# Column-tiled pairs of attention heads in layer 1, row ends shared between VectorE and GpSimd, and node sums laid into the last rows

## Chip, cores and metric

The kernel runs on one core of a Trainium2 chip. The metric is the device time of one execution in microseconds (us). Engines are called PE (matmul), PEld (weight load), DVE (VectorE), ACT (ScalarE), POOL (GpSimd) and SP (SyncE, here only a DMA queue).

## The reference, cut to what matters

Four layers on a graph of 2708 nodes with 256 features, each with a residual and a layer norm. The change is in layer 1, and in the passage from it to layer 2.

```python
# layer 1: masked attention, 4 heads of 64
h = (x @ W).reshape(n, heads, head_dim)
src = einsum('nhd,d->nh', h, a[:head_dim, 0]);  dst = einsum('nhd,d->nh', h, a[head_dim:, 0])
e = leaky_relu(src[:, :, None] + dst.T[None])          # slope 0.2
attn = softmax(where(adj > 0, e, -9e15), axis=-1)
out = einsum('nhm,mhd->nhd', attn, h).reshape(n, 256)
out = (out - mean) / sqrt(var + 1e-5) * gamma + beta
x = layernorm(x + out)
# layer 2 starts with: row statistics of the edge attention (min, then sum of exp, 3 heads),
#   node_support = (adj without diagonal) @ x, and a GRU cell on it
```

Nodes are cut into 22 row blocks of 128 (the last has 20 rows) and into six column groups (four of 512, one of 384, one of 276). "Row ends" are what is left of layer 1 for a row block when its sums are there: division by the softmax total, two normalisations, the residual. "Logits" are the small products of the finished rows that layer 2 needs. "Node sums" are the support matmuls of layer 2.

## The kernel before

For each column group and each head, DVE makes the unnormalised attention tile p (128 x 512), and PE multiplies it by the head's 64 features plus a 65th column of ones, which gives the softmax total. A scheduler fixes the order of every engine's instructions when the kernel is compiled; the engines then run their lists in order.

```python
for lo, hi in spans:                       # six column groups
    for h in range(H):
        acc = ps_acc.tile([P, 512], F32, tag="acc", name="acc")
        for c in range(NT):                # 22 chunks
            p = l1.tile([P, W], F32, tag="p", name="p", bufs=6)
            nc.vector.scalar_tensor_tensor(p[:, :w], fall_b[:, h, at : at + w], rise[:, c, h : h + 1],
                                           mask[:, c, at : at + w], ALU.max, ALU.mult)
            nc.tensor.matmul(acc[: HD + 1, :w], hs[c][:, h, :], p[:, :w], start=(c == 0), stop=(c == NT - 1))
            # ... every fifth chunk: one row block's logits
        # ... copy of the sums; after head 0: layer1_end of the group before, its elementwise work all on DVE,
        #     but for the power step of the norm, which is on GpSimd
```

The softmax here doesn't subtract the row's maximum and nothing guards it: scores larger than these inputs give would overflow.

## Time and profile before

2139.2 us is the median of three runs. The costliest groups that the change touches, from the page (name of the group, then busy us, mean ns of one, and idle time before it with what ended it):

```profile
L504 PE MATMUL acc<-p,h 128*65 128x512 f32 (+2 forms) x1056 | 417.8, 548 | 13.9 <-DVE p L500 12.8
L500 DVE SCALAR_TENSOR_TENSOR p<-fall_b,rise,mask 128x512 f32<-128x512 f32 (+2 forms) x528 | 354.4, 684 | 25.6 <-PE acc L504 2.1
```

Layer 1's matmuls take 418 us of PE, and DVE's p takes 354 us beside them. PE uses 65 of the 128 columns of its array. The prediction below shows the stages:

| stage of before | us | ends at |
|---|---|---|
| layer 1 proper | 466 | 728.5 |
| last rows, to the logits in DRAM | 26 | 755 |
| wait, then first pass of the row statistics | 34 | 789.3 |
| row statistics (66 passes on DVE) | 270 | 1059.5 |
| the rest | 1084 | 2144 |

### The profile page before, as it was taken

The page shows a single profiled execution, that of the slowest core. Times are in us where ns is not written, and L with a number is a line of the kernel's source. Part 1 is how long each engine was busy: PE and PEld are TensorE (multiplying, and loading weights), DVE is VectorE, ACT ScalarE, POOL GpSimd, SP SyncE. Part 2 cuts the span into 40 slices and gives each one's busy share as a digit, 9 for nine tenths or more (in the row PEclk, how much of TensorE's full clock was granted, in tenths as well). Part 3 has the DMA queues.
Part 4 walks back from the last instruction along what each step waited for, and adds up shares of the span by engine and source line. Part 5 has one row for each costly group of instructions (what it writes and reads, how often), then busy time and mean ns, then how long its engine had stood idle before and what let it go on. Part 6 is the DMA issues. An engine that isn't in the chain of part 4 may idle for free.

```text
span 2144.2 us, 18986 instructions
## 1 busy us (share of the span) xinstructions
PE 2058.3 (96%) x6618; PEld 1122.7 (52%) x6618; DVE 1342.5 (63%) x2721; ACT 694.3 (32%) x951; POOL 175.2 (8%) x286
## 2 busy tenths in 40 slices
PE   8999999999999889999889999999999999999997
PEld 7888633333234334445544444444444546678885
DVE  4333398989999739999856646646646557542111
ACT  0100145654111317767733333323323334320000
POOL 0111110120110110000000000000000000001111
PEclk9999999999999889999999999999999999999999
DMA  7344333331000297766380401301201101015452
GB/s 264 127 144 163 124 135 111 132 111 59 10 8 3 81 319 225 231 223 193 92 250 0 138 7 44 117 20 49 81 22 53 45 22 40 18 62 180 175 189 100
DMA packets 172564, 234.20 MB, mean 109 GB/s; under 512 B 18109, under 2 KB 149339, under 8 KB 161795
## 3 DMA queue, kind: packets, MB, share of 16 engines
q1 hardware_dynamic: 159738, 180.98, 26.5%
q0 software_dynamic: 9792, 47.51, 6.3%
q10 hardware_dynamic: 2928, 4.41, 0.6%
q8 instruction: 54, 0.88, 0.2%
q14 instruction: 52, 0.42, 0.1%
HBM read 221.63 MB, written 11.23 MB: 109 GB/s over the span
## 4 chain that ended last, share of the span: by engine, by line
PE 51%; DVE 5%; ACT 3%; issue 2%; SPq 2%; DMA 2%; POOL 0%; POOLq 0%; DVEq 0%; ACTq 0%
PE acc L801 20%; PE acc L178 9%; PE gate L584 8%; PE s L643 7%; PE gate L745 3%; PE pz L191 2%; ACT p L798 2%; SPq L170 2%; DVE p L795 2%; DMA blk<-in_adj_t_dram 1%; DVE z L682 1%; DVE p L799 1%; ACT z L687 1%; PE tr L141 0%; DMA strip<-in_adj_t_dram 0%
## 5 line engine op out<-in xcount | busy, mean ns | idle before, releaser
L801 PE MATMUL acc<-p,x 128*128 128x512 f32 (+2 forms) x1584 | 614.0, 544 | 6.2 <-DVE p L799 6.2
L801 PEld LDWEIGHTS acc<-p,x 128*128 128x128 f32 x1584 | 296.2, 190 | 298.7 <-issue 212.7
L504 PE MATMUL acc<-p,h 128*65 128x512 f32 (+2 forms) x1056 | 417.8, 548 | 13.9 <-DVE p L500 12.8
L178 PE MATMUL acc<-turn,strip 128*128 128x256 f32 (+1 forms) x1804 | 397.9, 379 | 1.4 <-DMA strip<-in_adj_t_dram 1.4
L500 DVE SCALAR_TENSOR_TENSOR p<-fall_b,rise,mask 128x512 f32<-128x512 f32 (+2 forms) x528 | 354.4, 684 | 25.6 <-PE acc L504 2.1
L178 PEld LDWEIGHTS acc<-turn,strip 128*128 128x128 f32 (+1 forms) x1804 | 331.2, 186 | 54.8 <-DMA strip<-in_adj_t_dram 1.8
L798 ACT ACTIVATE p<-p 128x512 f32<-128x512 f32 (+2 forms) x396 | 226.9, 578 | 401.5 <-DVE p L795 387.6
L799 DVE TENSOR_TENSOR p<-p,blk 128x512 f32<-128x512 f32 (+2 forms) x396 | 246.4, 626 | 169.8 <-ACT p L798 165.7
L504 PEld LDWEIGHTS acc<-p,h 128*65 128x65 f32 x1056 | 140.4, 139 | 256.7 <-issue 120.7
L687 ACT ACTIVATE z<-z,st 128x2708 f32<-128x2708 f32 (+1 forms) x66 | 168.4, 2552 | 102.7 <-DVE st L682 100.6
L682 DVE CUSTOM_DVE_ANT_0 z<-e_b,none 128x2708 f32<-128x2708 f32 (+1 forms) x66 | 195.4, 2967 | 0.3
L795 DVE TENSOR_SCALAR p<-st_b,e_col 128x512 f32<-128x512 f32 (+2 forms) x396 | 175.7, 448 | 15.8 <-PE acc L801 14.9
L134 POOL TENSOR_TENSOR bn_rs<-bn_ve,neg_half 128x1 f32<-128x1 f32 (+1 forms) x110 | 73.9, 674 | 1264.5 <-DVE bn_ve L132 1227.6
L643 PE MATMUL s<-blk,x 128*128 128x512 f32 (+2 forms) x416 | 165.5, 558 | 8.2 <-ACT supt L649 8.2
L584 PE MATMUL gate<-xt,whh 128*128 128x512 f32 (+2 forms) x288 | 123.5, 552 | 9.1 <-DMA xt<-xt 8.1
L643 PEld LDWEIGHTS s<-blk,x 128*128 128x128 f32 x416 | 80.9, 195 | 91.0 <-issue 69.3
L143 ACT COPY xt<-tr 128x256 f32<-128x256 f32 x66 | 23.8, 361 | 273.7 <-PE tr L141 266.7
L830 DVE SCALAR_TENSOR_TENSOR o<-acc,rdeg,o 128x256 f32<-128x256 f32 (+1 forms) x22 | 10.6, 483 | 144.3 <-PE acc L178 144.3
L584 PEld LDWEIGHTS gate<-xt,whh 128*128 128x128 f32 x288 | 55.8, 195 | 64.6 <-issue 45.0
L481 ACT ACTIVATE turn<-turn 128x2708 f32<-128x2708 f32 (+1 forms) x22 | 54.1, 2461 | 93.9 <-DMA turn<-in_adj_dram 93.9
L278 DVE TENSOR_SCALAR mask<-strip 128x2816 fp8e4<-128x2816 f32 (+3 forms) x37 | 36.7, 998 | 61.1 <-DMA strip<-in_adj_t_dram 60.9
L596 DVE SCALAR_TENSOR_TENSOR g_r<-g_r,g_h 128x512 f32<-128x512 f32 (+2 forms) x24 | 15.0, 626 | 92.2 <-ACT g_h L589 92.2
(147 smaller groups left out, 1400.6 us busy)
## 6 DMA issues: line engine op xcount, KB each, us to landing
strip<-in_adj_t_dram SPq DMA_DIRECT2D x41, 1408.0 KB, 6.1
blk<-in_adj_t_dram SPq DMA_DIRECT2D x189, 256.0 KB, 4.8
turn<-in_adj_dram SPq DMA_DIRECT2D x21, 1354.0 KB, 5.8
arow<-in_adj_dram POOLq DMA_DIRECT2D x21, 1354.0 KB, 7.0
st_b<-st_d SPq DMA_DIRECT2D x4, 1536.0 KB, 7.3
turn<-in_adj_t_dram SPq DMA_DIRECT2D x21, 256.0 KB, 7.0
blk<-in_adj_t_dram SPq DMA_DIRECT2D x36, 128.0 KB, 2.6
fall_b<-fall_d POOLq DMA_DIRECT2D x4, 1024.0 KB, 6.1
```

The lines of the kernel that those rows point to most:

```text
L134: nc.gpsimd.tensor_tensor(rstd[:n], ve[:n], neg_half[:n], ALU.pow)
L178: nc.tensor.matmul(acc, s[:, c, :n], rhs(c), start=(c == 0), stop=(c == NT - 1))
L500: nc.vector.scalar_tensor_tensor(p[:, :w], fall_b[:, h, at : at + w], rise[:, c, h : h + 1], mask[:, c, at : at + w], ALU.max, ALU.mult,)
L504: nc.tensor.matmul(acc[: HD + 1, :w], hs[c][:, h, :], p[:, :w], start=(c == 0), stop=(c == NT - 1))
L584: nc.tensor.matmul(g[:, :w], lt, rt, start=(q == 0), stop=(q == len(terms) - 1))
L643: nc.tensor.matmul(acc[f][:, :w], xs[c][:, f * P : (f + 1) * P], s[:, c - c0, :w], start=(c == 0), stop=(c == NT - 1),)
L682: nc.vector.tensor_tensor_reduce(out=z[:n], in0=e_b[:n, k, :], in1=none[:n], scale=-1.0, scalar=HIGHEST, op0=ALU.add, op1=ALU.min, accum_o ...
L687: nc.scalar.activation(z[:n], z[:n], AF.Exp, scale=-1.0, bias=st[:n, t, 0, k : k + 1], accum_out=den[:n])
L795: nc.vector.tensor_scalar(p[:, :w], st_b[:, k, :w], e_col[:, c, k : k + 1], 0.0, ALU.add, ALU.min)
L798: nc.scalar.activation(p[:, :w], p[:, :w], AF.Exp)
L799: nc.vector.tensor_tensor(p[:, :w], p[:, :w], blks[bi][:, c - c0, :w], ALU.mult)
L801: nc.tensor.matmul(acc[f][:, :w], xs[c][:, f * P : (f + 1) * P], p[:, :w], start=(c == 0), stop=(c == NT - 1),)
```

## The change

Its intent: use the idle half of the array, lighten DVE, and put waiting time to use. Two heads share the array as two 64-column tiles; two column groups share one p (1024 columns wide); the totals become four 32-column tiles of their own. Row ends become generators that advance one step per chunk, with the wide beta sum, the last normalisation, the epsilon steps and, within the loop, the split of u on GpSimd. In the last rows, the first column group's node sums run between the row ends.

```diff
+for q in range(H // 2):                                    # pairs of heads
+    acc = [ps_acc.tile([P, W], F32, tag="acc", name="acc") for _ in segs]   # two column groups
+    den = ps_acc.tile([P, W], F32, tag="acc", name="den")
+    def heads(c, ps, flags):
+        for s, (p0, ws) in enumerate(cols):
+            for i in range(2):
+                nc.tensor.matmul(acc[s][i * HD : (i + 1) * HD, :ws], hs[c][:, 2 * q + i, :HD],
+                                 ps[i][:, p0 : p0 + ws], **flags)
+    def totals(c, ps, flags):            # same loops; j = (2 * (s ^ q) + i) * CT
+                nc.tensor.matmul(den[j : j + CT, :ws], hs[c][:, 2 * q + i, HD + 1 - CT :], ...)
+    for c in range(NT):
+        # two p tiles of up to 1024 columns on DVE, then
+        for part in (heads, totals)[:: 1 if c % 2 == 0 else -1]:
+            part(c, ps, dict(start=(c == 0), stop=(c == NT - 1)))
+        step(c)                          # advances row ends (q == 0) or logits (q == 1)
...
 def layer1_end(pool, t, s, sums, dens):
+    nc.gpsimd.tensor_tensor(bx[:n], xs[t][:n], beta_b[:n], ALU.add)
+    yield
     # division, statistics, first half of the norm on DVE
+    nc.gpsimd.tensor_scalar(rstd[:n], mv[:n, 1:2], EPS, None, ALU.add)      # in rstd_of, twice
     nc.gpsimd.tensor_tensor(rstd[:n], rstd[:n], neg_half[:n], ALU.pow)
+    yield
+    nc.vector.scalar_tensor_tensor(o[:n], o[:n], rstd[:n], bx[:n], ALU.mult, ALU.add)
     # second statistics
+    nc.gpsimd.tensor_scalar(xs[t][:n], o[:n], mv[:n, 0:1], rstd[:n], ALU.subtract, ALU.mult)
...
+for k in range(len(ended) + 7):          # last rows
+    # one step of three row ends and of three logits, then
+    if k > 2:
+        next(ahead, None)                # one chunk of the first group's node sums
```

Further, row 0 and the first blocks of layer 2 are loaded early, and the logits come back from DRAM one head at a time.

## The prediction

> **What bounds the kernel now.** The change touches layer 1 (masked attention, four heads), its last rows, and the edge stage behind them, so I read those. A table of windows cut at their borders gives each engine's busy time; the chain of waits, which only reaches back to 728.9 us, confirms the borders. Rows are window, length, then busy us of PE, PEld, DVE, ACT, POOL:
>
> ```profile
> 262.40:728.50 466.10, 442.97 (x1366) 161.71 (x1367) 419.55 (x919) 177.55 (x151) 62.61 (x84) 0.99 0.20 69
> 728.50:755.00 26.50, 17.24 (x74) 6.88 (x73) 14.31 (x62) 8.04 (x11) 7.88 (x14) 0.77 0.60 159
> 755.00:787.60 32.60, 32.60 (x72) 14.20 (x71) 2.54 (x14) 0.00 (x0) 5.69 (x9) 0.92 1.05 330
> 787.60:1063.50 275.90, 261.37 (x667) 128.13 (x666) 267.51 (x337) 195.99 (x178) 11.11 (x21) 0.97 0.64 201
> ```
>
> Layer 1 proper takes 466 us, with PE 95% and DVE 90% busy. The last rows take 26 us and use no engine well. For the next 33 us DVE is idle. Then the edge stage keeps DVE at 97% and PE at 95%. To see who leads in layer 1 I took a stretch without row ends, first DVE, then PE:
>
> ```profile
> 302.95 13.63 DVE L500 SCALAR_TENSOR_TENSOR p<-fall_b,rise,mask 128x512 f32<-128x512 f32 x16
> 316.76 0.74 DVE L500 SCALAR_TENSOR_TENSOR p<-fall_b,rise,mask 128x512 f32<-128x512 f32 x1
> 317.42 0.28 DVE L528 SCALAR_TENSOR_TENSOR off<-offdiag,mask 128x128 f32<-128x128 f32 x1
> ```
> ```profile
> 302.75 22.48 PE L504 MATMUL acc<-p,h 128*65 128x512 f32 x52
> ```
>
> Sixteen p tiles take 13.63 us, 0.85 each, yet one alone occupies DVE only 0.66 (316.76 to 317.42). PE starts a matmul instruction every 0.43 us (22.48/52), and the trace has two of them per fp32 matmul (1056 for 528 calls), so a 512-column matmul costs 0.858. PE paces layer 1 while DVE has slack. Where row ends are mixed in, DVE falls behind: in the list of waits PE's weight loads wait 110.9 us for p.
>
> **What the Trainium skill says.** "TensorEngine Tiling (Array Packing)", Key Properties: column tiles load weights and multiply in parallel, and changing the mode drains the engine. The trace agrees for bf16: the edge logits already use 32-column tiles, and six matmuls (four of 512 columns, two of 384) fit into
>
> ```profile
> 707.90 0.56 PE L391 MATMUL pu<-turn,u_parts 128*32 128x512 bf16 x6
> 708.39 0.91 PE L504 MATMUL acc<-p,h 128*65 128x276 f32 x3
> ```
>
> The first four start 3 to 4 ns apart and the fifth 227 ns after the first. The drain is readable too: a 512-column fp32 matmul is followed by a tiled one after 522 ns instead of 429, so a mode change costs some 95 ns. No fp32 matmul of this trace is column-tiled.
> "TensorE: Matmul & The Clock Gate", Part 3, What overlaps and what doesn't: matmuls start and end in program order. Nothing in the trace contradicts it; for fp32, with two instructions per call, it is the danger (first rival).
> "SBUF — State Buffer", two separate sides: DVE with two SBUF inputs and GpSimd exclude each other for a whole instruction. The trace half agrees: the small GpSimd operations take 0.74 us (median) in layer 1 against 0.56 in the node stage, while DVE's p keeps its 0.66 pitch beside them.
>
> **The change part by part.**
>
> *Heads in pairs.* Before: 22 chunks x 4 heads x (4 x 0.858 + 0.640 + 0.460), the last two for the 384- and 276-column groups at the same rate, is 88 x 4.53 = 399 us of PE streaming. After: two heads share the array as two 64-column tiles, two groups of columns share one p, and the row totals, formerly the 65th column, become four 32-column tiles. If tiles run fully beside each other, a chunk of one pair in the two wide pairs of groups costs 2 x 0.858 for heads, 0.858 for totals and one mode change (the order alternates, so one per chunk): 2.67 us. Times 44 (22 chunks x 2 head pairs) x 2 is 235. In the last pair it costs 1.10 + 0.64 + 0.095 = 1.835, times 44 is 81. Sum 316: 83 us less.
>
> *DVE's p.* The pitch is 0.66 at 512 columns and 0.41 at 276 (689.96 to 690.37 in the timeline), which is 0.125 fixed plus 1.04 ns a column. At 1024 it is 1.19, at 660 it is 0.81: 176 x 1.19 + 88 x 0.81 = 281 us. In the first pair that is 105 us against PE's 117: PE still leads.
>
> *Row ends.* Today a row block costs DVE about 4.9 us: seven passes over 256 columns at a pitch of some 0.34, two statistics, about ten tiny operations at 0.07 to 0.15, and the diagonal. After: two passes, the beta sum, both epsilon steps and, inside the loop, the five-step split of u move to GpSimd, and the diagonal is one bf16 operation; some 2.5 us stay. Sixteen blocks run within the loop, eight in each later pair: 20 us each. DVE: 105 + 20 = 125 in the second pair, 72 + 20 = 92 in the last. PE's own row-end work (transposes, logits, edge parts) is about 2 us a block (443 busy less 399 streaming over 22), so 16 a pair, plus six more mode changes a block, 5 us. PE: 117 + 138 + 102 = 357. PE leads everywhere, DVE by 10% behind it. Waits: GpSimd gets, per block, four tiny operations and two wide ones in two chunks (5.3 us). At 0.74 to 1.0 for a tiny one behind the longer p and about 1.4 for a wide one (an estimate) that is 5.5 to 7 us, so it lags a little and DVE then waits for it: I allow 13 us. Layer 1: 370 instead of 466, **96 us less**.
>
> *Last rows.* Six blocks (3 + 3) instead of three, in 13 steps, each with four instructions of the first group's node sums (1.72 us) once three steps have passed: 10 x 1.72 + 6 x 2 + some 6 for the logits' chain, about 35 us instead of 26. But about 11 of 22 chunks (19 us) of sums are then done, against about 7 us before.
>
> *Edge stage.* The row statistics bound it: from 787.6 to 1063.5 DVE runs without a hole. They start when e_b has come, 33 us after the logits (755), because all of e_b and four block corrections come first:
>
> ```profile
> 786.80 0.29 DVE L173 TENSOR_TENSOR blk<-blk,offdiag 128x128 f32<-128x128 f32 x1 [0.61 <-DMA blk<-in_adj_t_dram]
> ...
> 789.27 2.98 DVE L682 CUSTOM_DVE_ANT_0 z<-e_b,none 128x2708 f32<-128x2708 f32 x1
> ```
>
> The changed program loads row 0 early, takes e_b one head at a time, and puts the corrections for the next group behind; a third of the bytes should land in some 7 us after the 6 us wait for e_d, so DVE starts 14 us after the logits instead of 33. First statistics: 35 + 14 = 49 us after layer 1's last matmul, against 61 now. The DVE work (276 us) is the same, and PE's remaining sums and gates (about 309 less 19, from the span 755 to 1063) just fit beneath it. **12 us less**. The loads of lwn from DRAM move nothing that bounds.
>
> Sum: 2139 - 96 - 12 = 2031 us.
>
> **The rivals.**
> 1. *fp32 pairs serialize.* Each fp32 matmul is two instructions into one tile. If PE issues strictly in order, the second blocks those behind it, and only the second half of one tile overlaps the first half of the next: one 0.43 slot per call, whatever the number of tiles. Then totals cost as much as heads: eight calls between two mode changes take nine slots, 3.96 us instead of 2.67, and PE needs 88 x 3.96 + 119 = 467 instead of 316. Layer 1 would be 510 us, the kernel some 2170. For: the skill's program order. Against: four tiles in the bf16 group start at once; and the order, which alternates heads with totals to save mode changes, and the work taken off DVE look like somebody met DVE as the next bound.
> 2. *GpSimd becomes the bound of the row ends.* It has no slack by the working above. At 8 us a block the 16 blocks cost 16 x 2.7 = 43 us, instead of my 13: about 2060.
> 3. *DVE becomes the bound.* 281 + 40 + blocked time. It is within 10% of PE; if mode changes are hidden this is what remains, 330 instead of 357: about 2005.
> 4. *The edge stage gives nothing*: PE has 290 us of work there and 276 are DVE's; if the block loads wait behind e_b, the 12 us vanish: about 2043.
>
> **Range and chances.** Rivals 2 to 4 spread the result from 2005 to 2060. Rival 1 would put it at 2170, between same and slower; I give it 15%, in part or in full. Hence 2032, 8 in 10 between 2000 and 2100; faster 0.84, within 2% 0.10, slower 0.06.
>
> **What would show it.** In the changed profile: heads matmuls of two tiles and totals of four tiles starting a few ns apart, a period of 2.7 us a chunk in the first pair (rival 1: 4.0); PE over 90% busy there and DVE about 90%; layer 1 some 370 us long; first z about 49 us after the last head matmul; last z about 276 us later. The prediction is wrong if the starts of a totals group are 0.43 apart, or if DVE shows long waits for bn_rs.

## The result, and the profile after

The changed kernel takes 2103.7 us (median of four runs, 2100.5 to 2104.7), the kernel before 2140.0 beside it. All outputs are right. The ratio is 0.983, with a 95% interval of 0.981 to 0.984. Ratios here are the mean time of one kernel's runs over that of the other's of the same rounds, so not quite the ratio of the medians quoted. The prediction was 2032 with a range of 2000 to 2100: the result lies just outside the range, and the gain of 36 us is a third of the 108 foreseen. The gain is clear of the noise, but smaller than 2%, for which the prediction gave a chance of 0.10.

The table of windows of the changed kernel, cut at its borders (window, length, then busy us of PE, PEld, DVE, ACT, POOL, the granted PE clock, DMA share, GB/s):

```profile
259.00:320.00 61.00, 60.42 (x340) 19.13 (x344) 53.86 (x44) 28.89 (x23) 9.46 (x10) 0.97 0.33 115
320.00:381.00 61.00, 60.83 (x356) 18.60 (x352) 54.60 (x45) 29.41 (x26) 3.43 (x5) 1.00 0.37 130
381.00:476.00 95.00, 93.03 (x433) 26.65 (x429) 71.50 (x112) 42.59 (x45) 66.40 (x91) 1.00 0.33 115
476.00:541.80 65.80, 65.80 (x399) 18.46 (x395) 56.40 (x54) 39.89 (x32) 7.48 (x16) 1.00 0.26 92
541.80:623.30 81.50, 75.85 (x437) 27.49 (x431) 54.45 (x112) 10.14 (x18) 50.30 (x81) 0.96 0.04 11
623.30:682.50 59.20, 59.20 (x406) 22.58 (x401) 39.15 (x51) 13.02 (x14) 7.71 (x19) 1.00 0.05 16
682.50:713.00 30.50, 24.08 (x84) 11.99 (x81) 16.47 (x73) 16.93 (x16) 21.30 (x37) 0.84 0.73 182
744.00:1020.00 276.00, 258.90 (x665) 126.18 (x664) 263.08 (x338) 195.30 (x176) 11.74 (x20) 0.98 0.66 209
```

Layer 1 is six stretches of 22 chunks: a pair of column groups by a pair of heads. The first two lines are such stretches without row ends: 61 us each. The third and fifth have the row ends of the pair before mixed in: 95 and 81.5 us. In the third, PE is 98% busy, although it has the same attention matmuls as in the second line. The sixth has few row ends and only 660 columns, where the prediction had 1.835 us a chunk, 40 us; it took 59. From its first p to the end of its last matmul layer 1 is now 425 us long (258.3 to 682.9), 41 less than the 466 before, where 96 less were foreseen. From there to the end of the last pass of the row statistics it is 337 us; before it was 331. That makes 35 us less. The two profiled runs differ by 41: the run of before that was profiled took 2146.0 us, 6 more than the median, and in the changed one layer 1 begins 4 us earlier and what follows the statistics is 1.6 us shorter.

**Do the tiles share the array?** PE's timeline in the first pair, which answers to the 52 matmuls of before at 0.43 each:

```profile
326.58 3.73 PE L611 MATMUL acc<-p,h 128*64 128x512 f32 x16
330.24 1.92 PE L620 MATMUL den<-p,h 128*32 128x512 f32 x16
```

Sixteen instructions of heads take 3.7 us, two at a time; sixteen of totals take 1.9, four at a time. In the records the tiles of one slot start 6 to 7 ns apart. Two chunks need 5.51 us, 2.76 each. One after another, they would need 32 x 0.43.

**What is different in the mixed stretches?** The same timeline in the second pair:

```profile
402.81 1.05 PE L620 MATMUL den<-p,h 128*32 128x512 f32 x2
403.79 1.07 PE L611 MATMUL acc<-p,h 128*64 128x512 f32 x2
404.79 1.06 PE L620 MATMUL den<-p,h 128*32 128x512 f32 x6
405.78 4.47 PE L611 MATMUL acc<-p,h 128*64 128x512 f32 x14
```

Here the groups have come apart. One totals tile (two instructions) goes alone and takes as long as four would. One heads tile goes alone, then the other three totals, then the heads left over. The order is the compiled one and no chance of this run: e_tail, e_braw and e_late below, whose edits lie behind these stretches, show the same 176 slots in stretch 2a. My reading is that the scheduler issued what needs the first head's p before the second head's p was expected. I counted the slots in the records (starts more than 0.2 us apart count as one slot each; a whole chunk has four of heads and two of totals) and the changes between heads and totals, for the six stretches (a few records are missing in the first):

| | 1a | 1b | 2a mixed | 2b | 3a mixed | 3b |
|---|---|---|---|---|---|---|
| changed kernel, us | 61.8 | 61.0 | 95.1 | 65.8 | 81.5 | 59.5 |
| slots (132 if whole) | 134 | 132 | 176 | 132 | 172 | 150 |
| changes (22 if whole) | 21 | 22 | 40 | 22 | 44 | 35 |

**Who waits for GpSimd?** From the list of waits (what waits, for whom, us in total, times, longest):

```profile
DVE o L519 <- POOL bn_rs L478: 46.8, 21, 10.2
ACT u L546 <- PE pm L542: 41.0, 17, 5.1
POOL u_parts L550 <- ACT u L546: 14.9, 9, 6.5
DVE braw L696 <- DMA braw<-in_L_gnn_edge_bhh_dram: 11.6, 1, 11.6
```

35.9 of the 46.8 us for bn_rs, the power step, are inside the loop. The longest of these waits in the timeline of all engines (start, duration, in brackets the idle time before and what ended it):

```profile
603.25 0.19 POOL L550 CAST u_parts<-u 128x3 bf16<-128x3 f32 x1 [6.47 <-ACT u L546]
603.39 0.57 POOL L478 TENSOR_TENSOR bn_rs<-bn_rs,neg_half 128x1 f32<-128x1 f32 x1
...
604.00 0.48 DVE L519 SCALAR_TENSOR_TENSOR o<-o,bn_rs,bx 128x256 f32<-128x256 f32 x1 [10.16 <-POOL bn_rs L478]
```

The epsilon step before it was done by 597, but the power step stands in GpSimd's order behind a split of u, which waits 6.5 us for ScalarE, which waits for PE. DVE stands for 10 us. PE itself was slow there: it had stood for 3.8 us (to 595.52), the granted clock is 0.5 from 593.9 to 600.7, and its groups are in pieces.

**And the edge stage?** DVE's timeline where the row statistics begin, to be held against the line at 789.27 in the prediction:

```profile
744.38 2.98 DVE L786 CUSTOM_DVE_ANT_0 z<-e_b,none 128x2708 f32<-128x2708 f32 x1 [9.46 <-DMA e_b<-e_d]
...
758.92 0.16 DVE L696 TENSOR_TENSOR braw<-braw 128x4 f32<-128x4 f32 x1 [11.56 <-DMA braw<-in_L_gnn_edge_bhh_dram]
...
759.21 2.97 DVE L786 CUSTOM_DVE_ANT_0 z<-e_b,none 128x2708 f32<-128x2708 f32 x1
```

The first pass comes 61 us after the end of layer 1's last matmul, not 49, and the second only 15 us after the first, because the GRU's biases stand between them in DVE's order, and DVE waits 11.6 us for their load. In the kernel before DVE waited for the same load too (9.2 us), but ahead of a longer wait for block loads (20.8 us), so that it cost nothing.

### The profile page after: what moved, and what is told of

Same layout as the page of the kernel before. It is cut to its first block, busy times and chain, and to the rows that moved or that the text cites.

```text
span 2102.9 us, 20961 instructions
## 1 busy us (share of the span) xinstructions
PE 2034.3 (97%) x7652; PEld 1096.3 (52%) x7652; DVE 1258.0 (60%) x2257; ACT 697.6 (33%) x973; POOL 274.2 (13%) x450
## 4 chain that ended last, share of the span: by engine, by line
PE 78%; DVE 8%; DMA 5%; ACT 3%; issue 2%; POOL 2%; SPq 1%; ACTq 0%; POOLq 0%; DVEq 0%
PE acc L911 22%; PE acc L178 18%; PE gate L717 9%; PE acc L611 9%; PE s L219 6%; PE den L620 5%; DVE z L786 3%; PE gate L855 3%; PE pz L191 2%; DMA turn<-in_adj_dram 2%; ACT p L908 1%; DVE p L905 1%; PE acc L373 1%; DMA braw<-in_L_gnn_edge_bhh_dram 1%; PE pm L290 1%
## 5 line engine op out<-in xcount | busy, mean ns | idle before, releaser
L629 DVE SCALAR_TENSOR_TENSOR p<-fall_b,rise,mask 128x1024 f32<-128x1024 f32 (+1 forms) x264 | 297.2, 1155 | 51.8 <-PE den L620 30.2
L611 PE MATMUL acc<-p,h 128*64 128x512 f32 (+2 forms) x1056 | 255.2, 558 | 1.6 <-DVE p L629 1.5
L135 POOL TENSOR_TENSOR bn_rs<-bn_ve,neg_half 128x1 f32<-128x1 f32 x66 | 39.0, 591 | 1058.4 <-DVE bn_ve L133 1058.4
L611 PEld LDWEIGHTS acc<-p,h 128*64 128x64 f32 x1056 | 82.3, 137 | 159.9 <-issue 147.3
L620 PE MATMUL den<-p,h 128*32 128x512 f32 (+2 forms) x1056 | 144.3, 552 | 0.3 <-DVE p L629 0.3
L717 PEld LDWEIGHTS gate<-xt,whh 128*128 128x128 f32 x288 | 55.8, 196 | 72.4 <-issue 53.2
L620 PEld LDWEIGHTS den<-p,h 128*32 128x32 f32 x1056 | 31.3, 108 | 90.3 <-issue 64.2
```

The source lines that it names most:

```text
L611: nc.tensor.matmul(acc[s][i * HD : (i + 1) * HD, :ws], hs[c][:, 2 * q + i, :HD], ps[i][:, p0 : p0 + ws], **flags,)
L620: nc.tensor.matmul(den[j : j + CT, :ws], hs[c][:, 2 * q + i, HD + 1 - CT :], ps[i][:, p0 : p0 + ws], **flags,)
L629: nc.vector.scalar_tensor_tensor(p[:, :w], falls[g // 2][:, 2 * q + i, :w], rise[:, c, 2 * q + i : 2 * q + i + 1], mask[:, c, at : at + w] ...
L717: nc.tensor.matmul(g[:, :w], lt, rt, start=(q == 0), stop=(q == len(terms) - 1))
```

## The experiments

There were four suspects: (A) cut groups on PE, (B) GpSimd, by its order or by its load, (C) GpSimd in the last rows, (D) the biases. Twelve kernels ran, in three sets; each set has its own runs of before (medians 2142.7, 2141.5, 2141.7), and the third (e_sw, e_late, c_spread, c_late) ran on another chip than the first two. "Stretch" is the time from one stretch's first p to the next one's, from the profile of one run.

### 1. Groups kept whole (e_runs)

```diff
+def chained(ins):       # this matmul comes after the one before it, in PE's order only
+    if chain:
+        tc.add_manual_dep(ins, chain[0].name, <NoSync>, reason="runs of tiles")
+    chain[:] = [ins]
 # in heads and in totals
-for i in range(2):
-    nc.tensor.matmul(...)
+for i in (1, 0):        # the head whose p comes last goes first
+    chained(nc.tensor.matmul(...))
```

> Edit: every heads and totals matmul of layer 1 is ordered behind the one before it, and in each group the head whose p comes last goes first, so that the scheduler can no longer cut the groups of tiles apart. Theory A (the schedule cut the groups, and each cut costs a mode change and leaves tiles alone on the array): the last pair's second stretch, which has few row ends (59.2 us for 22 chunks in the changed kernel), falls to about 45 us, the mixed stretches of the second and last pair by 3 to 8 us each; in all 15 to 28 us less than the changed kernel, 2076 to 2089. Rival B (tiles wait for p anyway, the cuts cost nothing): the stretch stays at 57 to 60 us and the total within 5 us of 2103.

Measured: 2087.6 us (2086.9 to 2090.1), ratio to before 0.975, so 16 us less than the changed kernel. The slots fell to 127, 132, 134, 132, 130 and 128, the changes to 21 to 23. The windows of layer 1's last four stretches:

```profile
385.10:480.40 95.30, 80.55 (x427) 23.12 (x423) 72.40 (x114) 44.53 (x44) 63.20 (x80) 0.89 0.31 109
480.40:547.60 67.20, 67.20 (x405) 17.50 (x401) 55.49 (x51) 38.30 (x32) 16.59 (x28) 1.00 0.26 92
547.60:618.70 71.10, 60.97 (x437) 23.59 (x431) 54.89 (x116) 10.22 (x18) 47.33 (x76) 0.93 0.04 12
618.70:668.40 49.70, 49.67 (x407) 18.32 (x401) 38.71 (x49) 13.32 (x15) 11.53 (x25) 1.00 0.07 21
```

The last pair lost 20 us (81.5 + 59.5 to 71.1 + 49.8). The second pair's mixed stretch did not get shorter at all, though PE's busy time in it fell from 93.0 to 80.6 us. In all four stretches PE's busy time fell by 35 us (293.9 to 258.4), and 16 of them reached the total. PE now waits in the mixed stretches, and its granted clock is 0.89. The timeline shows both:

```profile
414.02 1.94 PE L622 MATMUL acc<-p,h 128*64 128x512 f32 x8
418.31 3.05 PE L622 MATMUL acc<-p,h 128*64 128x512 f32 x8 [2.35 <-DVE p L640]
```

The same eight instructions take 1.94 us at 414 and 3.05 after a wait of 2.35 us. In the records the starts are 0.42 to 0.48 apart before the wait, and 0.64 to 1.00 apart from 418.8 to 422.1, 3.4 us long. "TensorE: Matmul & The Clock Gate", Part 1, What's actually happening, says that an activity window of about 3.4 us, running freely, halves the clock when PE was idle. The slow stretch agrees (granted clock 0.50 from 419.0 to 422.4); a hole of 2.35 us was enough for it here, while the one of 2.27 us before 413.03 was not followed by a lower clock. So theory A holds, at the low end of its range: where the cuts were gone, another limit stood right behind. The edit has two parts, the chain and the order of the two heads, which were not tried apart.

### 2. Split of u back on DVE (e_split)

```diff
-layer1_logits(l1, t, two_rows[t % 2], nc.gpsimd, 3)
+layer1_logits(l1, t, two_rows[t % 2], nc.vector, 3)
```

> Edit: inside the loop the five-step split of u into bf16 parts runs on DVE again; everything else on GpSimd stays. Theory A (the power step of bn_rs is stuck in GpSimd's order behind a split that waits for ScalarE and PE): DVE's waits for bn_rs in the loop fall from about 36 us to under 15, the two mixed stretches (95.0 and 81.5 us) lose 8 to 15 us each, total 2075 to 2090. Rival B (GpSimd is simply overloaded with wide operations): the waits stay above 25 us, and the total is within 6 us of 2103.

Measured: 2092.8 us (2092.1 to 2093.3), ratio 0.977, so 11 us less. Mixed stretches 93.3 and 75.4; DVE's wait for bn_rs in the loop is 23.8 us instead of 35.9, with a longest of 4.0 instead of 10.2. That is between the two expectations, and what the gain came from is only partly what I meant: the last pair's slots also fell (172 to 164, 150 to 137), and PE's busy time in the last four stretches by 6 us (293.9 to 287.7), so part of it is fewer cuts. And e_runs, where the split is still on GpSimd, has the same 23.7 us of these waits in the loop, with a longest of 2.4: the wait of 10 us went with the cut groups too.

### 3. Wide steps back on DVE, with and without the split (e_wide, e_sw)

```diff
-nc.gpsimd.tensor_tensor(bx[:n], xs[t][:n], beta_b[:n], ALU.add)
+wide.tensor_tensor(bx[:n], xs[t][:n], beta_b[:n], ALU.add)       # wide = nc.vector in the loop
 # likewise the two epsilon steps and the last tensor_scalar; e_sw adds the edit of e_split
```

> Edit: inside the loop the beta sum, both epsilon steps and the final normalisation run on DVE again (the power step and the split of u stay on GpSimd; the last rows are as in the changed kernel). If GpSimd's sheer load matters more than its order, this does more than moving the split of u did (2092.8 us): DVE's waits for bn_rs in the loop fall under 10 us and the total under 2090. If the power stuck behind the split is the main thing, waits of 4 us and more for bn_rs stay and the total is 2093 to 2101. In both cases the second pair's mixed stretch stays at 93 us or more, because there PE is 98% busy with cut groups.

Measured: 2120.2 us (2119.7 to 2123.1), ratio 0.991: 16 us more than the changed kernel, which neither side expected; the mixed stretches (101.8 and 85.9 us) are worse, too. In the loop DVE now waited for the power step at two places (12 and 25 us, together one more than before the edit). I took these waits, with the power step stuck behind the split, for the cause, and made e_sw to test that.

> Edit: in the loop both the split of u and the wide and epsilon steps run on DVE (e_split and e_wide together, nothing else; the power step alone of the row ends stays on GpSimd). If e_wide lost 17 us because DVE then stood twice per block for a power step that was stuck behind the split, the same move is harmless or helps once the split is gone: 2080 to 2095, at or below e_split's 2092.8, with waits for bn_rs under 10 us in the loop. If e_wide lost because DVE has no room for the work, the loss stays: 2105 to 2115.

Measured: 2107.1 us (2106.2 to 2107.8), ratio 0.983. The theory of the stuck power step fell: with the split gone, the wide steps still cost 14 us against e_split, and DVE still waits 33 us for bn_rs in the loop, where under 10 were expected. But "no room on DVE" fits little better, for DVE is only 74.0 us busy in the window of 95 us over the second pair's mixed stretch. The count of slots says more: 176, 136, 164, 137 in the last four stretches of e_split became 186, 140, 203, 143 in e_sw. PE's busy time in these stretches grew with them by 15 us (287.7 to 302.3), as much as the total; in e_wide it grew by 15 us as well (293.9 to 309.3). So the loss stands in PE's busy time, along with more cut groups. Why the scheduler cuts more of them is my reading: the more DVE has to do between two p tiles, the further apart it expects them. c_all2 below is a check.

### 4. Row ends of the last rows on DVE (e_tail)

The edit of e_wide, applied to the last rows alone.

> Edit: in the last rows alone, the beta sum, both epsilon steps and the final normalisation run on DVE again (the power stays on GpSimd). Theory A (GpSimd sets the 4.7 us between row blocks there): the blocks come every 2.5 to 3.3 us, the last rows take about 40 us instead of 50, total 2092 to 2096. Rival B (node sums on PE and the latency of each block's chain set it): the blocks stay 4 us or more apart and the total within 4 us of 2103.

Measured: 2099.5 us (2097.5 to 2103.2), ratio 0.980. The profile has the first pass of the statistics 55.4 us after layer 1's last matmul instead of 61.5, and the power steps of a block come some 3.8 us after those of the block before, not 4.7. GpSimd was a limit, with PE's node sums next behind it (PE is 25 of 29 us busy there). The total gained 4 us, of which the spread of the runs leaves little certain.

### 5. Biases early (e_braw)

```diff
-            b = gru_columns(ework, e_bih, e_bhh)       # in the edge stage
+                b = gru_columns(const, e_bih, e_bhh)   # before layer 1's last rows
```

> Edit: the biases of the edge GRU are loaded and combined before layer 1's last rows, into a buffer of their own. Theory A (DVE stands in order behind these biases after the first statistics pass): the second pass starts 3 us after the first instead of 15, the statistics end some 11 us earlier, total 2091 to 2094. Rival B (the second head's e_b has not come yet, or PE's sums take the gain back): the total falls by less than 5 us.

Measured: 2096.5 us (2093.2 to 2099.5), ratio 0.979. In DVE's timeline the second pass follows at once:

```profile
744.12 2.98 DVE L786 CUSTOM_DVE_ANT_0 z<-e_b,none 128x2708 f32<-128x2708 f32 x1 [9.54 <-DMA e_b<-e_d]
...
747.88 2.98 DVE L786 CUSTOM_DVE_ANT_0 z<-e_b,none 128x2708 f32<-128x2708 f32 x1 [0.77 <-DMA e_b<-e_d]
```

The last pass ends 7.4 us earlier than in the changed kernel. The missing 4 us are new waits of DVE: 1.3 us for more of e_b, 2.2 for ScalarE's sums, 0.9 for rows. Theory A, two thirds of it.

### 6. What a mode change costs (e_fixed)

```diff
-for part in (heads, totals)[:: 1 if c % 2 == 0 else -1]:
+for part in (heads, totals):              # on top of e_runs
```

> Edit: e_runs (groups kept whole, 2087.6 us) with heads always before totals, so two mode changes per chunk instead of one. If a change costs PE the 93 to 95 ns that the starts show, and PE sets the pace, the first pair's two stretches (62 us each of 22 chunks) grow by 2.1 us each and the total by 8 to 13 us, to 2096 to 2101. If changes are hidden (another engine sets the pace), everything stays within 3 us of e_runs.

Measured: 2092.6 us (2090.8 to 2095.6), ratio 0.978, 5 us above e_runs, less than the 8 to 13 expected. In the first pair, where PE sets the pace, the two stretches grew from 63.3 and 60.8 to 65.3 and 63.0: 2.1 us for 22 more changes, 95 ns each, as the starts show. In the other four stretches the sum moved by 0.4 us (283.3 to 283.7), up in one and down in another. In the mixed ones PE does not set the pace. In 2b and 3b it does, but there the logits' work, in other tile sizes, had split the runs already: the records of 2b have 45 changes of tile size in e_runs and 49 in e_fixed, against 22 and 44 in 1b.

### 7. The edits together (c_all, c_all2)

c_all is e_runs, e_split, e_tail and e_braw; c_all2 adds the wide steps on DVE in the loop.

> Four edits together: groups kept whole, split of u on DVE in the loop, last rows' wide and epsilon steps on DVE, edge GRU biases early. Singly they gave 15, 10, 4 and 7 us of the changed kernel's 2103: added, 2067. My theory says more than added, because in the second pair's mixed stretch (95 us) the cut groups and the stuck power step are two limits, each of which hides what the other costs: that stretch falls under 88 us, total 2050 to 2063. Rival: the edits took away the same waiting, and the total is 2070 to 2080.

> c_all with the beta sum, the epsilon steps and the final normalisation on DVE in the loop too; GpSimd keeps the power step alone. It adds some 0.9 us of DVE to each of 16 blocks, 14 us. If GpSimd's slowness still holds up the row ends in c_all, the mixed stretches get shorter than in c_all and the total falls by 3 to 10 us below it; if DVE is by then the leader of these stretches, they get longer by 3 to 7 us each and the total is above that of c_all.

Measured: c_all 2065.4 us (2062.5 to 2070.7), ratio 0.964; c_all2 2063.0 us (2058.8 to 2074.6), ratio 0.965. c_all is 38 us below the changed kernel, about the sum of the single gains, where I had expected more than that, and its second pair's mixed stretch is 91.9 us, not under 88. c_all2 is not certainly faster than c_all, since their runs overlap. But the edit that cost some 14 us (e_sw against e_split) and 16 us (e_wide against the changed kernel) where groups could be cut costs nothing once they are whole, and c_all2 has 132 slots in the mixed stretch. That is what the count of slots in experiment 3 led to expect. c_all2's windows of the same four stretches:

```profile
382.20:465.70 83.50, 73.16 (x418) 21.59 (x410) 76.30 (x143) 40.39 (x43) 21.09 (x30) 1.00 0.39 135
465.70:532.40 66.70, 66.63 (x410) 16.80 (x414) 59.65 (x97) 42.39 (x33) 2.84 (x5) 1.00 0.22 80
532.40:600.40 68.00, 55.56 (x418) 21.77 (x410) 59.78 (x144) 5.47 (x15) 16.31 (x23) 1.00 0.05 15
600.40:650.70 50.30, 50.29 (x422) 18.51 (x422) 42.04 (x91) 18.19 (x18) 1.31 (x5) 1.00 0.06 18
```

The mixed stretches are 83.5 and 68.0 us, the clock is back at 1.00 (0.91 in c_all's second pair, where PE was busy for 80.8 us and is now for 73.2), GpSimd is down from 63 to 21 us, and DVE is the busiest in the first and third lines. c_all2 with 2063 us beats both kernels.

### 8. Row ends spread out, and the fill taken away (c_spread, e_late, c_late)

c_spread, made from c_all2, begins a row end every third chunk, not every second, and the logits from the fifth chunk on (that line is not shown):

```diff
-if c % 2:
-    if q == 0 and ended:
+if True:
+    if q == 0 and (c % 3 == 1 or c == NT - 1) and ended:
```

> c_all2 with row ends begun every third chunk instead of every second, over the whole first stretch of a pair, and the logits from the fifth chunk of the second. If DVE's crowding (91% busy in the second pair's mixed stretch, 73% of 72 us plus, against PE's 88%) is what is left, the two mixed stretches (83.5 and 68.0 us) get 3 to 6 us shorter each and the second ones grow by 1 to 3: total 2050 to 2060. If the p tiles and the power step's latency set it, nothing moves: 2059 to 2066.

Measured: 2064.6 us (2063.2 to 2069.4), ratio 0.964, so nothing gained. The mixed stretch of the second pair went from 83.5 to 77.9 and its other one from 66.7 to 72.4: the sum stays at 150. The work moved, its amount did not; DVE's crowding within a stretch is not what is left.

e_late takes the first group's node sums from the last row block backwards, so that they can't fill the last rows:

```diff
-                next(ahead)
-                next(ahead)
 ...
-                    if k > 2:
-                        next(ahead, None)
 # in edge_sums: blocks in reverse order for the first group
```

> Edit: the node sums of the first group take the rows from the last block backwards and are emitted after the logits, so they can't fill the last rows; nothing else. If filling was worth what the prediction says (PE must have 12 us of sums out of the way to fit under DVE in the edge stage), the edge stage gets longer by 5 to 12 us and the total is 2106 to 2114. If the sums in front of the logits on PE delay them as much as they save later, the first statistics pass starts 3 to 6 us earlier and the total stays within 4 us of 2103.7.

Measured: 2115.9 us (2113.9 to 2117.5), ratio 0.987: 12 us more. The last pass of the statistics ended 2.7 us later than in the changed kernel, but so did layer 1 in this run (2.6 us); between the two nothing changed (337 us). The rest of the program took 10 us more after it: PE was behind with its sums. The first pass came only 1.2 us earlier after layer 1. The fill is worth what the prediction needed it for.

> c_spread with e_late's edit. If filling delays the logits and DVE leads the edge stage, the first pass comes earlier by 4 to 8 us and the total is 3 to 8 us below c_spread. If PE then leads the edge stage, the total is above c_spread by 0 to 8 us.

Measured: 2081.7 us (2077.8 to 2086.9), ratio 0.971, 17 us more than c_spread. The first pass came 51.3 us after layer 1 instead of 59.3, so the sums in front of the logits do delay them by 8 us; they cost more when they come later. That was expected above c_spread by 0 to 8 us, and it was twice that.

## Why the prediction was wrong, point by point

Against the prediction 72 us are missing: layer 1 is 425 us long and not 370, and what follows it lost 6 us where it was to gain 12.

**Heads in pairs: right.** fp32 tiles start 6 to 7 ns apart although a call is two instructions, and a chunk takes 2.76 us (predicted 2.67). The first slot after a mode change is another 0.02 to 0.05 us longer than the rest, which I had not counted. Rival 1, serial pairs, is refuted.

**DVE's p: right.** The median pitch of p in the first pair is 1.20 us, predicted 1.19. Rival 3, DVE as the bound, did not come about.

**Row ends: this step failed**, at "PE: 117 + 138 + 102 = 357". It takes the program's loops for the order in which PE runs them: whole groups, one mode change a chunk, six more a block. The compiled order has cut groups, and PE was busy for 415 us (121 + 159 + 135) and not 357. The records show 102 slots too many. As an estimate from the starts, 44 of them at 0.43 us and 58 at some 0.33 (384 columns) are 38 us of PE. e_runs, which keeps the groups whole, took 35 us off PE's busy time and 16 off the total. With whole groups the step's terms are nearly right: in c_all2 PE is busy for 139.8 us in the second pair (predicted 138) and 105.9 in the last (predicted 102).

**The 13 us for GpSimd: mis-sized.** The row ends themselves cost GpSimd 6.1 us a block, within the predicted 5.5 to 7. But the split of u, the DMA issues and the degrees share its queue, 66.4 us for 8 blocks, and a step that waits there holds up all behind it. DVE waited 35.9 us in the loop, the long waits for bn_rs that the prediction had named as a sign of being wrong. This is half of rival 2. Order and load seem to have a share each: moving the split cut the longest wait from 10.2 to 4.0 us (but whole groups alone to 2.4), and with the wide steps gone as well (c_all to c_all2, one profile each) the second pair's mixed stretch fell from 91.9 to 83.5 us, 7.6 of them PE's busy time at the higher clock. The wait was hidden in the second pair as long as the cut groups kept PE busy, and e_runs laid it bare, together with a lowered clock. In c_all2, with only the power step of the row ends on GpSimd, layer 1 is 392 us, 22 above the prediction.

**Last rows: mis-sized.** 35 us were predicted to the logits, and it took 48, to the last part at 731. GpSimd made the blocks come every 4.7 us (e_tail: 6 us of the way to the first pass), and the node sums stand in front of the logits on PE. In the changed kernel the sums delay the first pass by 1.2 us only (e_late); with the row ends on DVE it is 8 us (c_late). Only the sums are worth their price.

**Edge stage: half right.** From the logits (731) to the first pass (744.4) it is 13 us, predicted 14. "The DVE work is the same and PE's sums just fit" holds (e_late: without the fill 12 us more). What was missed is the wait for the biases, 11.6 us in DVE's order behind the first pass, which a longer wait had hidden before. e_braw got 7 us of it back. The predicted gain of 12 became a loss of 6: the first pass comes 12 us later than predicted, and the passes take 275.6 us, the wait included, against 270 from first to last pass in the kernel before (the 276 in the prediction was the window, with some work ahead of the first pass). Rival 4, no gain here, came true in size, but not by its cause: DVE waited only 0.9 us for block loads.

Two readings of the prediction were off without consequence: the 0.74 us of small GpSimd operations mixes two kinds, and the power step alone has a median of 0.89 in layer 1 against 0.56 in the node stage; and the fifth of the bf16 tiles starts 225 ns after the first, not 227.

What stays open: why c_all2 still needs 22 us more than predicted for layer 1, and which part of the waiting in the mixed stretches is GpSimd's and which the lowered clock's. PE has 9 us more work there (366 busy against 357); the rest is waiting in the mixed stretches (25 us against the 13 allowed), where c_spread shows that moving row ends about doesn't help.

## What to carry to other kernels

When a gain rests on instructions running beside each other, read the compiled order before predicting, and tie the group together if the scheduler may cut it, with the member whose data comes last in front (e_runs did both at once). Before moving a small step to an idle engine, look at what stands in front of it in that engine's queue and what that waits for. And when a stage gets shorter, look at every wait that the old stage hid: here the bias load cost nothing before and 11.6 us after.

## What the Trainium skill lacked or had wrong

- "TensorE: Matmul & The Clock Gate", Part 3, What overlaps and what doesn't, says that matmuls start and end in program order. In the changed kernel's last pair, where a 384-column totals tile is issued ahead of two 276-column ones, the second halves of the narrow tiles start at 628.798 and 628.805, before the wide tile's second half at 628.882. Between tiles, the order held only for the first halves.
- The same page and "TensorEngine Tiling (Array Packing)", Key Properties, don't say what fp32 does in column tiles. Here its two instructions per call overlap fully across tiles: four totals tiles start within 20 ns, their second halves 0.45 us later, also within 20 ns.
- "TensorEngine Tiling (Array Packing)", Key Properties, has the drain at a mode change but no figure. Here it is 93 to 95 ns between starts, and e_fixed gives 95 ns per change in the length of the first pair's two stretches.
- "TensorE: Matmul & The Clock Gate", Part 1, HAM oscillation — how this bites in real kernels, warns of gaps above some 3.4 us; the section after it tells of shorter idle times that lower the clock, without a length. In e_runs, after a hole of 2.35 us, the starts were up to 1.00 us apart instead of 0.43 to 0.52; after one of 2.27 us they were not.
- "SBUF — State Buffer", two separate sides, has the lock, and elsewhere on the page a GpSimd slowed by 1.5 times, but not by which DVE instruction. Here a subtract-and-multiply of 128 x 256 took 1.88 us on GpSimd on average in the second pair's mixed stretch, beside DVE's p, and 1.28 in the last rows, where no p runs (0.41 us on DVE in c_all2). Other causes of that difference were not ruled out.
